# Two transformer layers on one core: the second layer's first attention matrix turned by VectorE and moved by transfers instead of turned by TensorE, with its scores, its bias and an earlier decision moved along

## The chip, the core and the metric

The kernel runs on one core of a Trainium2 chip. The metric is the time of one execution in device microseconds (us). Of the kernel before, three executions gave 462.42, 463.27 and 463.12 us, so the median is 463.12 us. All times of day below ("at 238.47") are microseconds from the start of the profiled execution's span.

## What is computed

Two layers run one after the other on x of 2 sequences x 512 tokens x 512 features. Cut to what matters here:

```python
x = layernorm(x + linear_attention(x))     # 8 heads are read, D = 128
x = layernorm(x + quantised_ffn(x))        # gate, up, down, truncated to int8
# second layer, attention with one head of 128, for each sequence b
qkv  = x @ Wqkv + bqkv ; q, k, v = split(qkv)
attn = softmax((q @ k.T) / sqrt(128))      # 512 x 512 for each sequence
x = layernorm(x + (attn @ v) @ Wo + bo)
x = layernorm(x + swiglu_ffn(x))           # 512 -> 1376 -> 512
```

## The kernel before

**Layout.** A sequence is four tiles of 128 tokens (`xs[b][t]`, 128x512, tokens on partitions). A matmul contracts over partitions, so every time the features or the keys have to stand on partitions a tile is turned. The helper `transposed` (line 118) does that on TensorE: 16 matmuls of 128x128 against the identity into four PSUM tiles (line 128), and four copies to SBUF (line 130), by turns on ScalarE (ACT) and VectorE (DVE). A second way exists in the kernel, `move_squares` (line 286): VectorE first turns every 32x32 square of a tile in place (`nc.vector.transpose`, line 671), and then 16 transfers move the squares to their places, 64 KB each in runs of 128 bytes. Nine of them are issued by SyncE (SP), four by GpSimd (POOL) and three by ScalarE (line 294). The first layer uses it once, for the second sequence's rows (`xt1`).

**PSUM.** There are eight tiles of 128x512 (`psum`). Whoever writes a new one waits for the reader of the one whose place it takes.

**Order.** Instructions of an engine run in order. A scheduler orders all engines but POOL by the program and by what `tc.issue_after` ties; POOL keeps the order of the program. Five places matter here.

1. *Reading the first layer's memory* (lines 548 to 588, and the loop at 674). For each of the 8 token tiles, `read` makes eight matmuls into eight PSUM tiles (`po`, line 557). ACT copies out the denominators (561), VectorE takes their reciprocal (565), ACT scales three of the eight (570) and VectorE adds the other five to x (579). At turns 5 and 6 (counted from 0) TensorE also turns the first sequence's rows (`pt_f`, 275).
2. *The first decision.* Whether the feed-forward weights are ternary is decided by data: `total` sums the counts of misfits at turn 6, and `verdict` (lines 220 to 235) at turn 7 makes a matmul over partitions (`pf_up`, 224) and four small VectorE operations (226, 228, 231, 233). TensorE reads the flag (`branch`, 237), branches (732), and starts the feed-forward matmuls (`pg_f`, 735).
3. *The second attention's projections* (loop at 1012). For sequence 0 and then 1: the rows are turned (`pt_a`, `xt_a`), q and k are projected (`pqk`, 1026) and moved out by ACT (1031), and v is projected (`pv`, 1039) and moved out by VectorE (1043). Behind the turning of sequence 1 stand the splits of the next weights (`split_up`): ACT casts (939, 945) and VectorE differences (953, 954).
4. *Scores and probabilities* (`scores`, `exponentials`). Only after both sequences' projections come the four score matmuls of sequence 0 and the four of sequence 1 (`psc`, 1064), row maxima on VectorE (1070, 1071) and exponentials on ACT (1086).
5. *Turning and using the probabilities.* POOL adds the output bias `bo` to all eight x tiles (1100). TensorE turns sequence 0's probabilities (`pt_p`), `values` (1122) multiplies them by v, then sequence 1's are turned, and `output` (1138), `attended` (1143) and the norms follow.

Between 4 and 5 the kernel before reads:

```python
got, maxima = scores(0)
maxima(range(NT))
got1, maxima = scores(1)
maxima(range(NT - 1))
exponentials(0, got)
for b in range(B):
    for t in range(NT):
        nc.gpsimd.tensor_add(xs[b][t], xs[b][t], bo)
pt0 = transposed(probs[0][0], "p0")
with tc.issue_after(copies[-3].ins):
    scaled_max = maxima([NT - 1])
moved = exponentials(1, got1, {1: copies[-4], 2: copies[-2]})
```

Of the kernel before, what the change touches and what calls it, by code (L numbers as in the profile page):

```python
# [10 lines left out]
F32 = mybir.dt.float32  # L11
# [3 lines left out]
AF = mybir.ActivationFunctionType  # L15
ALU = mybir.AluOpType
# [3 lines left out]
P = 128  # L20
B, S, HID = 2, 512, 512
NT = S // P
NK = HID // P
NH, G, D = 8, 4, 128
# [6 lines left out]
SQ = 32  # L31
# [8 lines left out]
def kernel(  # L40
# [19 lines left out]
    nc = tc.nc  # L60
# [7 lines left out]
    small = ctx.enter_context(tc.tile_pool(name="small", bufs=4))  # L68
# [6 lines left out]
    wqkv = const.tile([P, NK, 3 * D], F32, tag="wqkv", name="wqkv")  # L75
    bv = const.tile([P, D], F32, tag="bv", name="bv")
# [5 lines left out]
    def psum(name):  # L82
        return ps.tile([P, 512], F32, tag="mm", name=name)
# [34 lines left out]
    def transposed(rows, name, in_turn=False):  # L118

        xt = xtp.tile([P, NK, S], F32, tag="xt", name=f"xt_{name}")  # L120
        done = None
        for k in range(NK):
            pt = psum(f"pt_{name}_{k}")
            with ExitStack() as tied:
                if in_turn and k:
                    tied.enter_context(tc.issue_after(done.ins))
                for t in range(NT):
                    done = nc.tensor.transpose(pt[:, ts(t, P)], rows[t][:, ts(k, P)], ident)
            move = nc.vector.tensor_copy if k == 1 or k % 2 > in_turn else nc.scalar.copy
            copies.append(move(xt[:, k, :], pt))  # L130
        return xt
# [209 lines left out]
    def query_tile(name):  # L341
        return wqp.tile([P, 2, HID], F32, tag="wq", name=name)
# [36 lines left out]
    with tc.tile_pool(name="a0w", bufs=1) as a0w, tc.tile_pool(name="a0", bufs=2) as a0:  # L379
# [293 lines left out]
        for i, (b, t) in enumerate(order):  # L673
            steps = read(b, t, lambda steps: norm_a0(i - 1, steps) if i else None)
            for _ in range((1, 1, 1, 1, 1, 1, 0, 0)[i]):
                check_up(*checks.pop(0))
            if i == 6:
                tot_up = total(counts_up[0], "up")
            elif i == 7:
                flag_up, eff_up = verdict(tot_up, sc_up, "up")  # L680
            if i == 5:
                parts, block = split(0)
                x2.append(parts)
                squares = xtp.tile([P, NT, HID], F32, tag="xt", name="squares")
            if i in (5, 6):
                for k in range(2):
                    block(2 * (i - 5) + k)
            if i > NT:
                turn_squares(i - 1)
# [251 lines left out]
    def weight_upper(w, h, name):  # L941

        upper(h, w)
        big = cutp.tile([P, 512], F32, tag="big", name=f"big_{name}")
        nc.scalar.activation(big, w, AF.Copy, scale=BIG)
        return big
# [24 lines left out]
    def take(n):  # L971
        got = free[:n]
        del free[:n]
        return got

    def split_up(j, room, bigs=(None, None)):

        c = turn[j]
        n = CHUNKS[c][1]
        for a in range(2):  # L980
            up_parts[j, a] = room[3 * a : 3 * a + 3]
            if n == P:
                w = gus[c][:, a].rearrange("p k i -> p (k i)")
            else:
                w = gus[c][a]
            if n == P or a == 0:
                done = weight_parts(w, up_parts[j, a], f"gu{j}_{a}", bigs[a])
                continue

            u, w = (v.rearrange("p (k i) -> p k i", k=NK) for v in (up_parts[j, a][0], w))  # L990
            h = u[:, :, : P // 2]
            upper(h, w)
            done = nc.vector.tensor_sub(u[:, :, P // 2 :], w, h.bitcast(F32))
        own = wffn.tile([P, 2 * n // P, 512], F32R, tag=f"gu{c}", name=f"ugu_{c}")
        free.extend(units(own))
        return done
# [8 lines left out]
    def table(func, behind):  # L1005

        with tc.issue_after(behind.ins):
            warm = small.tile([1, 1], F32, tag="warm", name=f"warm_{func.name}", bufs=1)
            nc.scalar.activation(warm, ln_eps[0:1], func)

    qkv = []
    for b in range(B):
        if b:
            xt_a1.append(transposed(xs[b], f"a1{b}"))
            with tc.issue_after(copies[-2].ins), tc.issue_after(copies[-1].ins):
                split_up(0, room0)
                split_up(1, room1[:6])
        xt = xt_a1[b]
        qk = []
        qk2 = query_tile(f"qk_{b}")  # L1020
        if b == 0:
            v2 = query_tile("v")
        for j in range(2):
            p = psum(f"pqk_{b}_{j}")
            for k in range(NK):
                nc.tensor.matmul(  # L1026
                    p, wqkv[:, k, ts(j, D)], xt[:, k, :],
                    start=(k == 0), stop=(k == NK - 1),
                )
            s = qk2[:, j, :]  # L1030
            moved = nc.scalar.activation(s, p, AF.Identity, bias=bqk[:, j : j + 1])
            qk.append(s)
        if b == 0:
            table(AF.Exp, moved)
        v = v2[:, b, :].rearrange("p (t d) -> p t d", t=NT)
        for t in range(NT):
            p = psum(f"pv_{b}_{t}")
            for k in range(NK):
                nc.tensor.matmul(  # L1039
                    p[:, :D], xt[:, k, ts(t, P)], wqkv[:, k, ts(2, D)],  # L1040
                    start=(k == 0), stop=(k == NK - 1),
                )
            nc.vector.tensor_add(v[:, t, :], bv, p[:, :D])
        qkv.append((qk[0], qk[1], v))


    room2 = room1[6:] + take(4)
    with tc.issue_after(moved.ins):
        bigs2 = [
            weight_upper(  # L1050
                gus[turn[2]][:, a].rearrange("p k i -> p (k i)"), room2[3 * a], f"gu2_{a}"
            )
            for a in range(2)
        ]

    probs = []

    def scores(b):

        qt, kt, _ = qkv[b]  # L1060
        got = []
        for t in range(NT):
            p = psum(f"psc_{b}_{t}")
            nc.tensor.matmul(p, qt[:, ts(t, P)], kt, start=True, stop=True)  # L1064
            got.append((p, small.tile([P, 1], F32, tag="mx", name=f"mx_{b}_{t}", bufs=8)))

        def maxima(tiles):
            for t in tiles:
                p, mx = got[t]
                nc.vector.reduce_max(mx, p, AX.X)  # L1070
                done = nc.vector.tensor_scalar_mul(mx, mx, -scale)
            return done

        return got, maxima

    def exponentials(b, got, behind={}):
        sums = small.tile([P, NT], F32, tag="sums", name=f"sums_{b}")
        row = []
        for t, (p, mx) in enumerate(got):
            if t % 2 == 0:  # L1080
                two = pair_tile(f"prob_{b}_{t}")
            e = two[:, t % 2, :]
            with ExitStack() as tied:
                if t in behind:
                    tied.enter_context(tc.issue_after(behind[t].ins))
                moved = nc.scalar.activation(
                    e, p, AF.Exp, bias=mx, scale=scale, accum_out=sums[:, t : t + 1]
                )
            row.append(e)
        probs.append((row, sums))  # L1090
        return moved

    got, maxima = scores(0)
    maxima(range(NT))
    got1, maxima = scores(1)
    maxima(range(NT - 1))
    exponentials(0, got)
    for b in range(B):
        for t in range(NT):
            nc.gpsimd.tensor_add(xs[b][t], xs[b][t], bo)  # L1100
    pt0 = transposed(probs[0][0], "p0")
    with tc.issue_after(copies[-3].ins):
        scaled_max = maxima([NT - 1])
    moved = exponentials(1, got1, {1: copies[-4], 2: copies[-2]})
    table(AF.Silu, moved)
    with tc.issue_after(scaled_max.ins):
        done = split_up(2, room2, bigs2)
    with tc.issue_after(done.ins):
# [6 lines left out]
    def values(b, pt, cuts):  # L1115

        ot = ot2[:, b, :]
        w = S // cuts
        for i in range(cuts):
            po = psum(f"pot_{b}_{i}")  # L1120
            for k in range(NT):
                nc.tensor.matmul(  # L1122
                    po[:, :w], qkv[b][2][:, k, :], pt[:, k, ts(i, w)],
                    start=(k == 0), stop=(k == NT - 1),
                )
            (nc.vector.tensor_copy if b else nc.scalar.copy)(ot[:, ts(i, w)], po[:, :w])
        ots.append(ot)
# [65 lines left out]
        return parts, done  # L1193

    values(0, pt0, 1)
    pt1 = transposed(probs[1][0], "p1")
    for t in range(NT):
        attended(0, t, output(0, t))
        norm_a1(0, t)
# [254 lines left out]
```

## Time and profile before

| what | value |
|---|---|
| median of three executions | 463.12 us |
| the profiled execution's own time | 462.71 us |
| its span, first to last instruction | 460.6 us |
| TensorE matmuls busy | 451.8 us, 98% of the span |
| VectorE busy | 343.1 us, 74% |
| ScalarE busy | 271.4 us, 59% |
| GpSimd busy | 107.1 us, 23% |
| TensorE's part of the chain that ended last | 92% |
| transfers of the core, mean | 76 GB/s |

The profiled execution took 2.1 us more than its span (462.71 less 460.6), and stands 0.4 us below the median. The chain that ended last is followed back from the last instruction; a piece of it is one stretch of time put down to what was then being waited for. In a line of the timeline the first two numbers are the start and the length in us, "x8" is a run of eight instructions merged, and the square brackets give the idle time before it and who ended it.

### The profile page before, as it was taken

How to read it: one execution, taken by the hardware profiler on the slowest of the kernel's cores; microseconds unless marked ns; L12 is line 12 of the kernel's file. 1: busy time of each engine (PE TensorE's matmuls, PEld its weight loads, DVE VectorE, ACT ScalarE, POOL GpSimd, SP SyncE). 2: the span in 40 equal slices, each digit the busy share in tenths (PEclk: the TensorE clock that was granted, in tenths of full speed). 3: DMA queues.
4: the chain of work that ended last, by engine and by line, in shares of the span. 5: the costliest groups of instructions: out<-in, count | busy, mean ns of one | idle time of the engine just before them, and what ended most of it. 6: DMA issues, size and time to landing. Idle time of an engine off the chain costs nothing.

```text
span 460.6 us, 5889 instructions
## 1 busy us (share of the span) xinstructions
PE 451.8 (98%) x1945; PEld 340.4 (74%) x1945; DVE 343.1 (74%) x663; ACT 271.4 (59%) x516; POOL 107.1 (23%) x144
## 2 busy tenths in 40 slices
PE   9999999999899999999999999999999999999994
PEld 8887754344488888888776678888888888888884
DVE  4976857676967878847979899795655878998632
ACT  4778995547467964466755743574755668442101
POOL 0301106566540069101374032000000000020111
PEclk9999999999999999999999999999999999999999
DMA  8999980000038001121580000000000000001101
GB/s 295 395 266 306 183 307 1 0 3 0 2 68 268 5 3 48 47 92 38 196 323 0 2 0 2 0 0 1 0 1 0 1 2 0 1 23 46 38 32 46
DMA packets 21652, 35.03 MB, mean 76 GB/s; under 512 B 9840, under 2 KB 10736, under 8 KB 21616
## 3 DMA queue, kind: packets, MB, share of 16 engines
q1 hardware_dynamic: 18464, 29.54, 18.3%
q0 software_dynamic: 1280, 4.46, 5.0%
q10 hardware_dynamic: 1872, 0.56, 0.5%
q8 instruction: 22, 0.36, 0.3%
q14 instruction: 14, 0.11, 0.1%
HBM read 31.40 MB, written 2.10 MB: 73 GB/s over the span
## 4 chain that ended last, share of the span: by engine, by line
PE 92%; DVE 3%; issue 2%; ACT 1%; POOL 0%; POOLq 0%; DVEq 0%
PE pm L1244 17%; PE po L557 9%; PE pq L502 9%; PE pg_f L735 9%; PE pu_f L735 9%; PE pc L1244 8%; PE pdm L1332 8%; PE pd_f L794 4%; PE pdc L1332 4%; PE pqk L1026 3%; PE pv L1039 2%; PE pot L1122 1%; PE po L1138 1%; PE psc L1064 1%; PE pmw L543 1%
## 5 line engine op out<-in xcount | busy, mean ns | idle before, releaser
L557 PE MATMUL po<-mw,q 128*128 128x512 f32 x128 | 57.0, 598 | 0.6 <-ACT den L561 0.4
L557 PEld LDWEIGHTS po<-mw,q 128*128 128x128 f32 x128 | 22.9, 189 | 33.1 <-issue 18.6
L146 POOL TENSOR_TENSOR rstd_f<-mv_f,ln_eps 128x1 f32<-128x1 f32 x15 | 4.4, 294 | 173.7 <-DVE mv_f L1347 133.2
L1244 PE MATMUL pm<-r,ugu 128*128 128x512 f32 x152 | 37.7, 389 | 0.0
L1244 PE MATMUL pm<-r,it_early 128*128 128x512 f32 x144 | 36.6, 392 | 0.0
L1244 PEld LDWEIGHTS pm<-r,ugu 128*128 128x128 f32 x152 | 28.5, 188 | 5.9
L170 ACT ACTIVATE ta_f<-y_f,below_half 128x512 int8<-128x512 f32 (+1 forms) x22 | 15.9, 721 | 28.5 <-DVE y_f L158 28.2
L1244 PEld LDWEIGHTS pm<-r,it_early 128*128 128x128 f32 x144 | 27.0, 188 | 6.0 <-issue 0.5
L579 DVE SCALAR_TENSOR_TENSOR x<-po,den,x 128x511 f32<-128x511 f32 x40 | 29.8, 745 | 2.0
L1254 DVE SCALAR_TENSOR_TENSOR ev_q<-pm,ev_q 128x512 f32<-128x512 f32 x27 | 18.6, 688 | 14.1 <-PE pm L1244 14.1
L574 POOL TENSOR_TENSOR y<-y,y 128x511 f32<-128x511 f32 x16 | 21.1, 1318 | 26.0 <-PE po L557 21.0
L761 DVE SCALAR_TENSOR_TENSOR it_f<-tb_f,ta_f 128x512 fp32r<-128x512 int16 (+1 forms) x22 | 15.2, 690 | 13.8 <-ACT tb_f L171 13.8
L735 PE MATMUL pg_f<-xh,tu 128*128 128x512 f32 x88 | 24.1, 395 | 1.1 <-ACT den L561 1.1
L1253 ACT ACTIVATE ev_q<-pc 128x512 f32<-128x512 f32 x27 | 16.0, 594 | 14.1 <-PE pc L1244 14.0
L735 PE MATMUL pg_f<-xl,tu 128*128 128x512 f32 x88 | 23.6, 390 | 0.0
L735 PE MATMUL pu_f<-xh,tu 128*128 128x512 f32 x88 | 23.5, 389 | 0.0
L735 PE MATMUL pu_f<-xl,tu 128*128 128x512 f32 x88 | 23.5, 389 | 0.0
L561 ACT ACTIVATE den<-po,den_eps 128x1 f32<-128x1 f32 x64 | 13.9, 278 | 12.5 <-PE po L557 12.4
L349 POOL TENSOR_SCALAR td<-wd,inv_down 128x512 fp32r<-128x512 f32 x11 | 19.8, 1821 | 2.0 <-DVE inv_down L206 2.0
L1134 ACT ACTIVATE x<-x,off_f,rstd_f 128x512 f32<-128x512 f32 x7 | 5.7, 816 | 24.7 <-POOL off_f L1133 24.7
L794 PE MATMUL pd_f<-td,it_f 128*128 128x512 f32 x88 | 20.3, 389 | 0.0
L735 PEld LDWEIGHTS pg_f<-xh,tu 128*128 128x128 f32 x88 | 16.1, 188 | 4.5 <-ACT den L561 1.2
(362 smaller groups left out, 1151.5 us busy)
## 6 DMA issues: line engine op xcount, KB each, us to landing
gu<-in_gu SPq DMA_DIRECT2D x20, 512.0 KB, 6.8
wd<-in_wd SPq DMA_DIRECT2D x20, 256.0 KB, 5.2
wo<-in_wo SPq DMA_DIRECT2D x8, 512.0 KB, 8.3
wo<-in_wo POOLq DMA_DIRECT2D x8, 512.0 KB, 9.9
wq<-in_wq SPq DMA_DIRECT2D x8, 256.0 KB, 4.9
x<-in_x SPq DMA_DIRECT2D x7, 256.0 KB, 4.7
out<-x SPq DMA_DIRECT2D x7, 256.0 KB, 2.0
wqkv<-in_wqkv SPq DMA_DIRECT2D x1, 768.0 KB, 21.6
```

Of the source, the lines that this page charges most:

```text
L170: nc.scalar.activation(a[:n], y, AF.Relu, bias=below_half[:n])
L349: eng.tensor_scalar(out, w, factor, None, ALU.mult)
L502: done = nc.tensor.matmul(p, w, x, start=(start and i == 0), stop=(i == len(todo) - 1), skip_group_check=not start,)
L557: nc.tensor.matmul(po, qs[b][h0 + j][:, ts(t, P)], mw[:, h0 + j, :], start=True, stop=True,)
L574: nc.gpsimd.tensor_add(ys[0][:, :LAST], ys[0][:, :LAST], y[:, :LAST])
L579: steps.append(nc.vector.scalar_tensor_tensor(x[:, :LAST], four[j][:, :LAST], d, x[:, :LAST], ALU.mult, ALU.add))
L735: nc.tensor.matmul(pp[a], t[:, a, i % NK, :], x2[b][i], start=(i == 0), stop=(i == 2 * NK - 1),)
L794: nc.tensor.matmul(pd, inter[b][c][:, ts(t, P)], td[c].bitcast(F32R), start=(c == 0), stop=(c == last),)
L1244: nc.tensor.matmul(p, w, x, start=(left[id(p)] == begun[id(p)]), stop=(left[id(p)] == 1))
L1253: nc.scalar.activation(ev, pc, AF.Copy, scale=CROSS)
L1254: nc.vector.scalar_tensor_tensor(ev, pm, MAIN, ev, ALU.mult, ALU.add)
L1332: nc.tensor.matmul(p[:, :w], got[j // 4][1][kind][:, j % 4], down_parts[j][kind][:, cols], start=(j == 0 and kind == kinds[0]), stop=(j == ...
```

## The change

Sequence 0's scores, maxima and exponentials are made inside the projection loop, straight behind its v. VectorE turns each exponential tile in 32x32 squares, and POOL adds the bias to sequence 0's x tiles there. When the loop comes to sequence 1, `move_squares` is called behind its q and k: 16 transfers write `pt0`. TensorE no longer turns sequence 0's probabilities, so 16 of its transposes and the four copies behind them are gone. Sequence 1's probabilities are still turned by TensorE.

Sequence 1's bias is no longer added by POOL. A POOL copy of one column of `pt0` (`landed`) waits for the move, and behind it POOL issues four transfers that add `bo` from device memory onto the x tiles, 256 KB each.

`values` reads the probabilities with the tokens in four pieces of 128, a row step apart, as `pt0` now has them; `pt1` is given the same form by a view. The ties that interleaved sequence 1's maxima and exponentials with the copies of `pt_p` are gone. And `total` and `verdict` of the first decision come one turn earlier, at turns 5 and 6.

```diff
-            if i == 6:
+            if i == 5:
                 tot_up = total(counts_up[0], "up")
-            elif i == 7:
+            elif i == 6:
                 flag_up, eff_up = verdict(tot_up, sc_up, "up")
...
-        if b == 0:
+        if b:
+            pt0 = fp.tile([P, NT, NK, P], F32, tag="it10", name="pt_p0", bufs=1)
+            move_squares(squares, pt0)
+            pt0 = pt0.rearrange("p t k i -> p k t i")
+        else:
             table(AF.Exp, moved)
...
         qkv.append((qk[0], qk[1], v))
+        if b == 0:
+            got, maxima = scores(0)
+            maxima(range(NT))
+            exponentials(0, got)
+            squares = fp.tile([P, NT, HID], F32, tag="it00", name="squares_p0", bufs=1)
+            for t in range(NT):
+                nc.vector.transpose(squares[:, t, :], probs[0][0][t])
+                nc.gpsimd.tensor_add(xs[0][t], xs[0][t], bo)
...
-    got, maxima = scores(0)
-    maxima(range(NT))
-    got1, maxima = scores(1)
-    maxima(range(NT - 1))
-    exponentials(0, got)
-    for b in range(B):
-        for t in range(NT):
-            nc.gpsimd.tensor_add(xs[b][t], xs[b][t], bo)
-    pt0 = transposed(probs[0][0], "p0")
-    with tc.issue_after(copies[-3].ins):
-        scaled_max = maxima([NT - 1])
-    moved = exponentials(1, got1, {1: copies[-4], 2: copies[-2]})
-    table(AF.Silu, moved)
+    got, maxima = scores(1)
+    scaled_max = maxima(range(NT))
+    table(AF.Silu, exponentials(1, got))
+
+    landed = small.tile([P, 1], F32, tag="landed", name="landed", bufs=1)
+    nc.gpsimd.tensor_copy(landed[2 * SQ : 3 * SQ], pt0[2 * SQ : 3 * SQ, NK - 1, NT - 1, P - 1 :])
+    for t in range(NT):
+        nc.gpsimd.dma_start(xs[1][t], bo_in.to_broadcast([P, HID]), accum_op=ALU.add)
...
                 nc.tensor.matmul(
-                    po[:, :w], qkv[b][2][:, k, :], pt[:, k, ts(i, w)],
+                    po[:, :w].rearrange("p (t i) -> p t i", i=P), qkv[b][2][:, k, :],
+                    pt[:, k, ts(i, NT // cuts)],
                     start=(k == 0), stop=(k == NT - 1),
                 )
...
-    pt1 = transposed(probs[1][0], "p1")
+    pt1 = transposed(probs[1][0], "p1").rearrange("p k (t i) -> p k t i", t=NT)
```

More of the change, by code (lines that the diff above doesn't have):

```diff
@@ L1009, in table @@
             nc.scalar.activation(warm, ln_eps[0:1], func)
-    qkv = []
-    for b in range(B):
[L1013 to L1020, printed above, removed]
-        if b == 0:
[L1022 to L1035, printed above, removed]
-        for t in range(NT):
[L1037 to L1054, printed above, removed]
     probs = []
@@ L1091, in exponentials @@
         return moved
-    got, maxima = scores(0)
-    maxima(range(NT))
-    got1, maxima = scores(1)
-    maxima(range(NT - 1))
-    exponentials(0, got)
-    for b in range(B):
-        for t in range(NT):
-            nc.gpsimd.tensor_add(xs[b][t], xs[b][t], bo)
-    pt0 = transposed(probs[0][0], "p0")
-    with tc.issue_after(copies[-3].ins):
-        scaled_max = maxima([NT - 1])
-    moved = exponentials(1, got1, {1: copies[-4], 2: copies[-2]})
-    table(AF.Silu, moved)
+    qkv = []
+    for b in range(B):
+        if b:
+            xt_a1.append(transposed(xs[b], f"a1{b}"))
+            with tc.issue_after(copies[-2].ins), tc.issue_after(copies[-1].ins):
+                split_up(0, room0)
+                split_up(1, room1[:6])
+        xt = xt_a1[b]
+        qk = []
+        qk2 = query_tile(f"qk_{b}")
+        if b == 0:
+            v2 = query_tile("v")
+        for j in range(2):
+            p = psum(f"pqk_{b}_{j}")
+            for k in range(NK):
+                nc.tensor.matmul(
+                    p, wqkv[:, k, ts(j, D)], xt[:, k, :],
+                    start=(k == 0), stop=(k == NK - 1),
+                )
+            s = qk2[:, j, :]
+            moved = nc.scalar.activation(s, p, AF.Identity, bias=bqk[:, j : j + 1])
+            qk.append(s)
+        if b:
+            pt0 = fp.tile([P, NT, NK, P], F32, tag="it10", name="pt_p0", bufs=1)
+            move_squares(squares, pt0)
+            pt0 = pt0.rearrange("p t k i -> p k t i")
+        else:
+            table(AF.Exp, moved)
+        v = v2[:, b, :].rearrange("p (t d) -> p t d", t=NT)
+        for t in range(NT):
+            p = psum(f"pv_{b}_{t}")
+            for k in range(NK):
+                nc.tensor.matmul(
+                    p[:, :D], xt[:, k, ts(t, P)], wqkv[:, k, ts(2, D)],
+                    start=(k == 0), stop=(k == NK - 1),
+                )
+            nc.vector.tensor_add(v[:, t, :], bv, p[:, :D])
+        qkv.append((qk[0], qk[1], v))
+        if b == 0:
+            got, maxima = scores(0)
[5 more added lines that the diff above has]
+                nc.gpsimd.tensor_add(xs[0][t], xs[0][t], bo)
@@ new lines @@
+    room2 = room1[6:] + take(4)
+    with tc.issue_after(moved.ins):
+        bigs2 = [
+            weight_upper(
+                gus[turn[2]][:, a].rearrange("p k i -> p (k i)"), room2[3 * a], f"gu2_{a}"
+            )
+            for a in range(2)
+        ]
+    got, maxima = scores(1)
[3 more added lines that the diff above has]
+    nc.gpsimd.tensor_copy(landed[2 * SQ : 3 * SQ], pt0[2 * SQ : 3 * SQ, NK - 1, NT - 1, P - 1 :])
```

## The prediction

> **What bounds the kernel now.** Parts 1 and 2 of the page come first.
>
> ```profile
> PE 451.8 (98%) x1945; PEld 340.4 (74%) x1945; DVE 343.1 (74%) x663; ACT 271.4 (59%) x516; POOL 107.1 (23%) x144
> ...
> PEclk9999999999999999999999999999999999999999
> ```
>
> TensorE (PE) is busy throughout at its full clock, so only TensorE's own instructions and its holes set the time. The second view is the chain that ended last (start, length, what), around the two places that the change touches.
>
> ```profile
> 114.72 1.73 PE po L557 x4
> 120.66 1.28 ACT y L570 x3
> 123.14 2.10 PE pg_f L735 x8
> ...
> 236.72 1.75 PE pt_a L128 x16
> 238.47 6.87 PE pqk L1026 x16
> 245.34 3.57 PE pv L1039 x32
> 248.91 6.87 PE psc L1064 x16
> 255.78 1.75 PE pt_p L128 x16
> 257.53 3.44 PE pot L1122 x8
> 260.96 1.75 PE pt_p L128 x16
> ```
>
> From 236.72 to 262.7 each piece begins where the last ended, all of them TensorE's: what is taken from its queue there is gained. At the first place there is a hole before 123.14. The timeline shows it.
>
> ```profile
> 114.93 0.18 DVE L565 RECIPROCAL den<-den 128x4 f32<-128x4 f32 x1 [1.47 <-ACT den L561]
> ...
> 121.72 0.28 PE L224 MATMUL pf_up<-tot_up,ones 128*128 128x1 f32 x2
> 122.31 0.96 DVE L233 TENSOR_SCALAR eff_up<-sc_up,yes_up,no_up 128x2 f32<-128x2 f32 x1
> 123.14 1.18 PE L735 MATMUL pg_f<-xh,tu 128*128 128x512 f32 x4 [1.14 <-ACT den L561]
> ```
>
> The flag's path fills the hole: matmul at 121.72, comparisons on VectorE (DVE), a flag load on TensorE's sequencer at 122.4, a branch, and the next matmul 1.42 after the first. All times below are the old trace's.
>
> **Part 1, the decision a turn earlier: -1.0.** `pf_up` moves in front of the transposes at 113.68 and costs 0.14 of TensorE there. Its five VectorE operations (L226, 228, 231, 233, 717) took 1.34 from 122.04 to the reciprocal at 123.38. They now start about 0.32 behind `pf_up`, at 114.0, and end at 115.34. VectorE idled up to 114.93 anyway (the 1.47 in the first line), so it is only 0.41 late. It has no pause until 121.5, so what is queued behind, the additions of `po` (L579), frees PSUM 0.41 later. The addition that ended at 117.21 now ends at 117.62, and the fourth `po` matmul, which waits for its place, starts at 117.7; five matmuls of 0.86 (two instructions of 0.43) end the turn at 122.0 instead of 121.72. The flag has been ready for 7 us by then. Its load need not wait for the matmuls in front: the third decision's load ran between 197.5 and 197.9 while `pd_f`, the work behind its branch, began at 200.81 without a hole. So `pg_f` starts near 122.1: 1.0 gained. If the load hides only in part, 0.4; with no lateness on VectorE, 1.4.
>
> What follows the earlier start? Sequence 1's feed-forward begins at 145.0 and reads blocks that ACT and VectorE cut from 141.71 to 144.94. A start at 144.0 still finds the upper cuts (done at 143.88), and needs the first lower cut 0.9 later. No new wait; behind it the chain is TensorE's up to 224.
>
> **Part 2, the transposes: -1.75.** One `pt_p` run goes: 16 x 0.109 = 1.75, on the path in full. Its four copies leave ACT and VectorE.
>
> **Part 3, scores in front of sequence 1's rows: +0.5.** Matmuls only change places: `psc` of sequence 0 at 236.72 to 240.16, the rows' transposes to 241.91, then `pqk`. But in the built order ACT does exponentials 0 and 1, copy 0 of the rows, exponentials 2 and 3, copy 2; VectorE squares 0, maxima 2 and 3, squares 1, copy 1, squares 2 and 3, copy 3. `pqk` reads the copies one by one, 0.86 apart. Maximum 0.68 and scaling 0.15 (L1070, L1071), exponential with its sum 0.88 (L1086), one square run 0.71 (L671), copies 0.59 on ACT and 0.69 on VectorE (L130):
>
> - maximum 0 from 237.7, exponential 0 to 239.5, squares 0 to 240.2;
> - maxima 2 and 3 to 241.4, squares 1 to 242.2, copy 1 to 243.0; exponentials 2 and 3 to 243.3, copy 2 to 243.9;
> - squares 2 and 3 to 244.25, copy 3 to 244.9.
>
> `pqk` wants copy 1 at 242.77 and has it at 243.05: 0.3. Copy 3 costs 0.1 to 0.2 more. I take 0.5. Bounds: 0 (if the hand-overs are quicker) and 1.4. The upper one comes from the next lines.
>
> ```profile
> 235.74 11.75 POOL L1100 TENSOR_TENSOR x<-x,bo 128x512 f32<-128x512 f32 x8
> 241.35 1.65 DVE L954 TENSOR_TENSOR it_early<-it_early 128x512 fp32r<-128x512 f32 x1
> 248.56 0.68 DVE L954 TENSOR_TENSOR it_early<-it_early 128x512 fp32r<-128x512 f32 x1
> ```
>
> While GpSimd (POOL) adds the bias, the same VectorE operation takes 1.65 instead of 0.68. Four of the eight adds stay, from 235.74 to about 240.8, beside squares 0: at 1.65 that costs 0.94 more. But the L671 at 112.75 and 120.79 took 0.71 beside POOL adds, and L671 with POOL idle 0.69 to 0.71; so 0.71 it is.
>
> **Part 4, the move of the squares: 0, with 2.2 to spare.** The same move stands in the trace:
>
> ```profile
> L294 SPq DMA_DIRECT2D xt_f<-squares x9: 627/644/1197, 132.2 to 138.8; - x9
> L294 POOL DMA_DIRECT2D xt_f<-squares x4: 666/676/992, 132.7 to 135.0; - x4
> L294 ACTq DMA_DIRECT2D xt_f<-squares x3: 643/654/735, 132.1 to 133.5; - x3
> ...
> DMA to landing us min/median/max: 2.1/3.6/4.9
> ```
>
> Squares done at 132.02 (L671), first reader at 141.71: 9.7 at most, set by SP's nine issues. From 244.25 that is 253.9. The weight loads on the same queues are out of the way: SP's last issue ends at 232.35 and lands some 8.2 later (the median of its six loads there), by 240.6. New is ACT: its three issues stand behind its eight casts and around the two `qk` evictions, the first at about 249.0, the others after 250.0. SP's ninth waits, in the built program, for ACT's first to land: 251.2, so it issues by 251.9 and lands by 254.1. `pot` starts when `psc` of sequence 1 ends, 240.16 + 1.75 + 6.87 + 0.5 + 3.57 + 3.44 = 256.3. Without that cover each us late costs one. ACT's issues (3 x 0.65) and POOL's (4 x 0.68) lie beside TensorE's work.
>
> The Trainium skill ("VectorE: DVE Perf Modes", "The three transpose paths" and "Rules for kernel authors") says that VectorE turns only 32x32 blocks and advises TensorE for a 128x128 transpose where PSUM will do; taken as a rule for this case the sum would be no gain, not -1.75, but it weighs the operation alone, not which engine bounds. The skill ("DMA: Bandwidth & Descriptors", "Specifications") asks for 512 bytes or more for full transfer rate and the runs here have 128, while its section "Why small descriptors are slow (HBM only)" exempts moves within SBUF; by either, the 9.7 above already holds the price, so the sum stays.
>
> **Part 5, the strided `values`: 0.** No row has 512 columns in four pieces. Nearest: `pv`, 128 columns an instruction, 0.112 each (3.57 / 32), 0.446 for 512 against 0.430 (3.44 / 8). So 0 to +0.13; contiguous runs of 512 bytes are nearer to 0.
>
> **Part 6, sequence 1's bias: 0.** `landed` holds POOL until 254.1; its next work is the norm at 265.97 (L146). Four issues of 0.86, 1.27 apart as in the L606 run at 44.12, end by 259. The POOL loads of part 6 landed in 9.9 at twice the size: x tiles complete from 264.3 to 268.1. `attended` reads them (L1143) at 270.56, 271.42, 272.28 and 275.21, now about 1.2 earlier in this stage's terms. Nothing waits; a shortfall would cost its own length.
>
> Behind `pot` VectorE and ACT have less than before (copies gone, maxima done), and the holes between 274 and 298, VectorE's row splits, stay.
>
> **Sum.** -1.0 - 1.75 + 0.5 = -2.25. The span goes from 460.6 to 458.35, the profiled execution from 462.71 to 460.46. That execution was 0.4 below the median, so I forecast 463.12 - 2.25 = **460.9**; its own range is 460.0 to 461.7 (parts 1 to 3 at their nearer ends).
>
> **Rivals.**
> 1. *The decision gains nothing.* The part of the change that doesn't do what it says: VectorE's lateness reaches the last `po` and the load stays exposed. For it: L233 took 0.96 beside a POOL add and a POOL add runs at 113.94 too. Against it: the third decision. -1.25: 461.9.
> 2. *The row copies are late.* Squares 0 at 1.65 gives +1.4 in part 3, and the decision only 0.4: -0.4 - 1.75 + 1.4 = -0.75: 462.4, within what can't be told from none.
> 3. *The move lands late: slower.* Place: the first `pot` matmul, waiting for SP's ninth transfer, which waits for ACT's first. If the eight splits run at 1.65, as five did in this trace, ACT's casts, which wait for them, let the first ACT issue out at about 254.4 (+5), SP's ninth lands near 259.5 and `pot` waits 3.2; `qk` of sequence 1 is late for `psc` by some 2 of these. With the rest of the sum: -2.25 + 3.3 = +1.05, 464.2. It decides from 5.4 us of lateness on (2.2 to spare, 2.25 gained, 0.93 to count as slower); below 4.45 the change still gains. For it: a queue of waits that the earlier move, issued by idle engines, never had. Against: POOL has stopped adding by 241, and rows without POOL show 0.68.
>
> **Chances.** Forecast 0.56, rival 1 0.14, rival 2 0.14, rival 3 0.16. A difference under 0.2% (0.93 us) can't be told from none here. So faster (below 462.2) 0.70, same 0.14, slower 0.16. The range reaches from the forecast with all of part 1 and no stall (-3.2: 459.9, and 459.8 with the spread of the runs) past rival 2 to the middle between it and rival 3: 463.0.
>
> **What would show it.** Right: one `pt_p` run fewer, no piece but TensorE's between `psc` and `pot`, `pg_f` directly behind the last `po`, and holes of some 0.3 in the second `pqk`. Wrong: `pot` waiting for a transfer, `psc` for ACT's `qk`, L671 over 1 us, or L1143 waiting for POOL's queue.

## The result and the profile after

The changed kernel takes **465.59 us** (median of six executions, 465.43 to 466.13), the kernel before beside it 463.19 (six, 462.42 to 464.31). The ratio is 1.0051, 95% interval 1.0038 to 1.0065: slower by 2.4 us where a gain of 2.25 was forecast. The profiled execution took 466.13, with a span of 464.4, where that of before had 460.6.

The two rows of the page that were shown of before, now of the kernel after:

```profile
PE 456.6 (98%) x1929; PEld 338.2 (73%) x1929; DVE 340.1 (73%) x665; ACT 270.6 (58%) x514; POOL 107.2 (23%) x149
...
PEclk9999999999999999999999999999999999999999
```

TensorE has 16 instructions fewer, as meant, at the same clock. Yet it is busy 4.8 us longer (456.6 for 451.8). That one row holds the case: the time was not lost in a wait.

The chain of the kernel after at the first place (start, length, what):

```profile
115.00 0.13 PE pf_up L224 x2
...
115.49 0.92 DVE eff_up L233
...
116.58 0.10 DVE den L565
...
118.85 4.53 PE po L557 x10
123.38 1.84 PE pg_f L735 x8
```

The hole is gone: the decision is made on VectorE by 116.58, seven us ahead, and `pg_f` follows the last `po` at once. From the chain's first `po` (64.08, in before 62.91) to its first `pg_f` it took 59.30 instead of 60.23.

The same chain around the second attention:

```profile
226.62 1.75 PE pt_a L128 x16
...
238.80 3.44 PE psc L1019 x8
242.24 1.75 PE pt_a L128 x16
243.98 7.03 PE pqk L1063 x16
...
254.59 3.44 PE psc L1019 x8
258.02 3.43 PE pot L1129 x8
261.45 1.75 PE pt_p L128 x16
```

One `pt_p` run is gone, `pot` follows `psc` without a wait, and the second `pqk` takes 7.03 instead of 6.87. From the first `pt_a` to the end of the first `pot` it is 34.83 us (226.62 to 261.45), in before 36.58 (224.38 to 260.96); 0.15 of these 1.75 are the first `pt_a` (1.75 for 1.90), so the change itself gained 1.6: 1.75 less the 0.16.

So both places gained, 0.93 and 1.6, and yet the span grew by 3.8. The loss is in pieces that nobody touched. One piece of the chain in the kernel before:

```profile
200.81 4.99 PE pd_f L794 x22
```

and the same 22 matmuls in the kernel after:

```profile
202.37 5.13 PE pd_f L794 x22
```

A run of 22 fp32r matmuls of 128x512 takes 5.13 instead of 4.99: 5.13 / 22 = 233 ns from start to start instead of 227. This holds nearly everywhere, also in the feed-forward of the first layer (an L735 run of eight: 1.85 or 1.86, in before 1.81), far ahead of the attention that was changed, and behind it (`pdm` x22: 5.11, in before 4.99). Matmuls of full fp32 kept their time (`psc`, eight in 3.44). From the first `pg_f` to the second layer's `pt_a` the kernel after needs 103.24 us instead of 101.24, and from the attention's last `po` (end at 275.27, in before 274.78) to the end of the last matmul 183.47 instead of 179.94: 5.5 us lost, more than was gained.

### The profile page after: what moved, and what is told of

The parts are those of the page before. It is cut to its first block, busy times and chain, and to the rows that moved or that the text cites. A ratio compares the mean times of both kernels' runs of the same rounds, so it can differ in the third digit from the quotient of the medians.

```text
span 464.4 us, 5879 instructions
## 1 busy us (share of the span) xinstructions
PE 456.6 (98%) x1929; PEld 338.2 (73%) x1929; DVE 340.1 (73%) x665; ACT 270.6 (58%) x514; POOL 107.2 (23%) x149
## 4 chain that ended last, share of the span: by engine, by line
PE 92%; DVE 3%; issue 2%; DMA 1%; ACT 1%; SPq 0%; POOL 0%; POOLq 0%; DVEq 0%
PE pm L1252 18%; PE po L557 10%; PE pq L502 9%; PE pg_f L735 9%; PE pu_f L735 9%; PE pc L1252 8%; PE pdm L1340 8%; PE pd_f L794 4%; PE pdc L1340 4%; PE pqk L1063 3%; PE pv L1080 2%; PE pot L1129 1%; PE po L1146 1%; PE psc L1019 1%; PE pmw L543 1%
## 5 line engine op out<-in xcount | busy, mean ns | idle before, releaser
L735 PE MATMUL pg_f<-xh,tu 128*128 128x512 f32 x88 | 24.8, 404 | 0.0
L735 PE MATMUL pu_f<-xh,tu 128*128 128x512 f32 x88 | 24.1, 396 | 0.0
L735 PE MATMUL pu_f<-xl,tu 128*128 128x512 f32 x88 | 23.9, 393 | 0.0
L735 PE MATMUL pg_f<-xl,tu 128*128 128x512 f32 x88 | 23.8, 392 | 0.0
L1252 PE MATMUL pc<-r,ugu 128*128 128x512 f32 x72 | 19.7, 395 | 0.0
```

Of the source, the lines that this page charges most:

```text
L735: nc.tensor.matmul(pp[a], t[:, a, i % NK, :], x2[b][i], start=(i == 0), stop=(i == 2 * NK - 1),)
L1252: nc.tensor.matmul(p, w, x, start=(left[id(p)] == begun[id(p)]), stop=(left[id(p)] == 1))
```

## The experiments

**Theory A** after this comparison: the new tile `landed` is the cause, by its place in memory. In the built program it takes 32 bytes of each partition, and 361 tiles allocated behind it, weights and activations of the fp32r matmuls among them, lie 32 bytes higher than in the kernel before. **Theory B**: the new order, the transfers or POOL's work slow the matmuls. **Theory C**: it was the chip or the execution. Ratios below are to the kernel before on the same chip, whose median was 463.2 to 463.6.

### same

The kernel before once more.

> The kernel before, unchanged. Theory A (addresses): untouched fp32r matmuls of 512 columns start 227 ns apart as in the first profile of it (pd_f x22 in 4.99 us), about 463.2 us. Theory C (the chip or the execution gave the slow pace): about 232 ns apart here too, and then every kernel of this call shows it.

Measured: 464.19 us, span 462.1. `pd_f` x22 took 4.99 again, so C falls. The span is 1.5 longer than in the first profile; 1.05 of it lies between the first `po` and the first `pg_f`, where one `po` waited 0.5 for ACT's `y` (L570). One profile alone thus tells stages of the first layer to no better than about 1 us.

### aligned

```diff
-    landed = small.tile([P, 1], F32, tag="landed", name="landed", bufs=1)
+    landed = small.tile([P, 16], F32, tag="landed", name="landed", bufs=1)
...
```

POOL's copy in the next line now names the tile's first column.

> The changed kernel with the tile landed 64 bytes a partition instead of 4. In the built programs every engine has the same instructions in the same order; only the 361 tiles that are allocated behind landed lie 64 bytes higher than in the kernel before, where the change put them 32 bytes higher. Theory A (the 32 bytes slow the matmuls): the pace returns to 227 ns (pd_f x22 in 4.99 us instead of 5.13), and what is left is the saving of the decision (0.93) and of the transposes (1.75): 463.2 - 2.7 = 460.5 us. Theory B (the new order, its transfers or POOL's work slow the matmuls): no change, 465.6 us.

Measured: 465.74 us, ratio 1.0042 (1.0028 to 1.0056); `pd_f` x22 5.13. My size for theory A was wrong: 64 bytes are no better than 32. By itself this run favours B.

### shift

```diff
+    landed = small.tile([P, 1], F32, tag="landed", name="landed", bufs=1)
+    nc.gpsimd.memset(landed, 0.0)
     pt0 = transposed(probs[0][0], "p0")
```

> The kernel before, with one 4-byte tile added (landed, cleared once by POOL behind its bias adds); nothing else. The same 361 tiles lie 32 bytes higher. Theory A: the pace goes to 231 to 235 ns from the first quarter of the kernel on, some +5 to +6 us: 468 to 469 us. Theory B: 463.2 us, no difference.

Measured: 469.77 us, ratio 1.0130 (1.0113 to 1.0147): +6.2 us. The same piece of the chain in this kernel:

```profile
203.66 5.13 PE pd_f L794 x22
```

To a hundredth the piece of the kernel after (and `pdm` x22 has 5.11 here too), in a program that is the kernel before plus four bytes a partition. So the slow pace does not need B, and A stands, but not with a boundary of 64 bytes.

Setting the addresses of the operands in the built program beside the pace gave **theory D**. In the kernel before, the two operands of 1,264 of the 1,371 fp32r matmuls of 512 columns start a multiple of 512 bytes apart, those of the other 107 an odd multiple of 256 (the expectation of reuse below says 512 of all). In the kernel after, 811 of them stand 32 bytes off this. A long stretch where both operands had moved by 32 ran at 227 ns (1.81 / 8, from 310.19 to 315.6 on the chain), and those where only one had moved at 231 to 235.

```profile
310.19 0.91 PE pc L1252 x4
311.10 1.81 PE pm L1252 x8
```

So what counts is where the moving operand and the stationary operand lie *to each other*.

### reuse

```diff
-    landed = small.tile([P, 1], F32, tag="landed", name="landed", bufs=1)
+    landed = small.tile([P, 1], F32, tag="off", name="landed")
```

> The changed kernel with landed put into a place that the kernel already has (the small tile off of the norms), so that no tile of an fp32r matmul lies elsewhere than in the kernel before; the same instructions in the same order as the changed kernel. Theory D (the pace depends on where the moving operand and the stationary operand lie to each other: 227 ns where their addresses differ by a multiple of some power of two above 64 bytes, as all do in the kernel before by multiples of 512, and some 232 ns otherwise): pace 227, time 463.3 - 0.9 - 1.75 = 460.6 us or a little below. Theory B (the change's own order or transfers slow the matmuls as well): between 462 and 465.6.

Measured: **460.54 us**, ratio 0.9927 (0.9905 to 0.9948). The piece of its chain:

```profile
200.61 4.99 PE pd_f L794 x22
```

The same instructions in the same order as in the kernel after, 5 us faster by the place of one small tile. With this B is out.

### pad128 and pad512

```diff
-    landed = small.tile([P, 1], F32, tag="landed", name="landed", bufs=1)
+    landed = small.tile([P, 32], F32, tag="landed", name="landed", bufs=1)    # pad512: [P, 128]
...
```

> The changed kernel with landed of 128 bytes a partition; 361 tiles lie 128 bytes higher than in the kernel before, instructions and order as in the changed kernel. Theory D with a period of 128 bytes: pace 227, 460.6 us. With a period of 256 or more: 231 to 234 ns, about 465.6.

> As before with 512 bytes a partition. Theory D: 227 ns and 460.6 us, since every difference of addresses is again a multiple of 512. If any added memory costs, whatever its size: about 465.6.

Measured: pad128 465.40, ratio 1.0040 (1.0025 to 1.0055), `pd_f` x22 5.11; pad512 **459.91**, ratio 0.9922 (0.9895 to 0.9949), `pd_f` x22 4.99. It is not added memory that costs, but an addition that is no multiple of the period, and the period is above 128.

### micro

> Leaves the whole computation out: 13 stretches of 48 fp32r matmuls of 128x512, four stationary blocks in turn, nothing beside them; the output is one moved-out result for each tile, not the layers'. The stationary operand lies 0, 4, 16, 32, 64, 128, 256, 512, 96 bytes off the moving operand's place modulo 512; then both 32 off, the moving alone 32 off, the moving by turns 0 and 32 off; then 0 again. Theory D: 227 ns from start to start at 0, 512, 0 again and both 32 off (10.9 us a stretch of 48), 230 to 235 ns (11.1 to 11.2 us) at 32, 64, 96, moving alone and by turns; 4 and 16 as 32, 128 and 256 tell the period. If other engines' accesses are needed for the slow pace: 227 ns in all of them.

The timeline of TensorE in this kernel (start, length, and the tile named after the offset; in the `b_` stretch both operands are 32 bytes off, in `m_thirtytwo` the moving one alone, in `m_turns` every second moving one):

```profile
19.06 11.32 PE L83 MATMUL s_four<-mov,sta 128*128 128x512 f32 x48
30.21 11.36 PE L83 MATMUL s_sixteen<-mov,sta 128*128 128x512 f32 x48
41.41 11.35 PE L83 MATMUL s_thirtytwo<-mov,sta 128*128 128x512 f32 x48
52.60 11.36 PE L83 MATMUL s_sixtyfour<-mov,sta 128*128 128x512 f32 x48
63.80 11.32 PE L83 MATMUL s_onetwoeight<-mov,sta 128*128 128x512 f32 x48
74.96 11.05 PE L83 MATMUL s_twofivesix<-mov,sta 128*128 128x512 f32 x48
85.84 11.05 PE L83 MATMUL s_fivetwelve<-mov,sta 128*128 128x512 f32 x48
96.73 11.07 PE L83 MATMUL b_thirtytwo<-mov,sta 128*128 128x512 f32 x48
107.64 11.36 PE L83 MATMUL m_thirtytwo<-mov,sta 128*128 128x512 f32 x48
118.84 11.20 PE L83 MATMUL m_turns<-mov,sta 128*128 128x512 f32 x48
129.88 11.40 PE L83 MATMUL s_ninetysix<-mov,sta 128*128 128x512 f32 x48
141.12 11.05 PE L83 MATMUL s_again<-mov,sta 128*128 128x512 f32 x48
```

Read the starts, since the ends overlap: a stretch's start to the next one's, over 48. At 256 bytes (85.84 - 74.96) / 48 = 227 ns, at 512 and with both operands moved 227 also; at 32 bytes (52.60 - 41.41) / 48 = 233, at 64 also 233, at 128 232.5; the offsets of 4, 16 and 96, by the same reckoning, 232, 233 and 234. By turns it is 230, between the two. No other engine takes part but for one copy a stretch, so it is TensorE's own two operands. (The very first stretch, at offset 0, began with matmuls 427 ns apart and is left out; the last one, `s_again`, repeats it and takes 11.05, as at 256 and 512.)

This settles the cause. A period of 256 bytes fits every offset that was tried, and theory D's price fits: in the kernel after some 1,330 consecutive pairs of such matmuls were 3 to 6 ns above 227 on average by their class of offset, 6.5 us in all, and shift measured 6.2.

Not all of this falls on operands that lie apart. In 530 of these pairs the moving operand lies 0 or 256 from its own weights and from the next ones, as in the kernel before, and yet they start 230 ns apart on average: 1.6 of the 6.5 us. Most of them stand in short runs between the others. Micro shows that the pace can take some matmuls to settle after a change of place: the first starts of `b_thirtytwo` are 230, 224, 231, 236, 228, 233, 231 and 226 ns apart, and from there on nearly all 227 or 226 (in `s_again` only the first, 231, stands out). The same series is in the kernel after: of the `pc` and `pm` from 297.02 on whose two operands both stand 32 off, the starts are 230, 236, 228, 233, 231, 226, 227 and 227 apart. That the 1.6 us are this settling is likely, not shown.

### decision, squares, poolbias

These three size the parts of the change with the addresses of the kernel before. decision is the kernel before with the decision alone a turn earlier:

```diff
-            if i == 6:
+            if i == 5:
                 tot_up = total(counts_up[0], "up")
-            elif i == 7:
+            elif i == 6:
```

> The kernel before, with the first decision alone one turn earlier; all addresses as before. From the trace of the changed kernel: the time from the first po to the first pg_f falls from 60.23 to 59.30 us, so 463.2 - 0.9 = 462.3 us. If the gain is given back behind it: 463.2.

Measured: 462.35 us, ratio 0.9976 (0.9965 to 0.9986): -1.1 us. squares is the kernel reuse with these two lines turned back.

> The kernel reuse (addresses as in the kernel before) with the first decision back at turns 6 and 7: parts 2 to 6 of the change alone. If these parts bring what they are forecast, less the stall that was 0.16 in the trace of the changed kernel: 463.5 - 1.75 + 0.15 = 461.9 us, and the difference to reuse is the decision, 0.9 to 1.2. If the two parts are not additive (a hole that only appears without the other): outside 461.5 to 462.3.

Measured: 461.08 us, ratio 0.9952 (0.9938 to 0.9966): -2.2 us, with 1.6 to 2.9 in the interval. The parts add up: 0.9976 x 0.9952 = 0.9928, and reuse has 0.9927.

```diff
-    landed = small.tile([P, 1], F32, tag="off", name="landed")
-    nc.gpsimd.tensor_copy(landed[2 * SQ : 3 * SQ], pt0[2 * SQ : 3 * SQ, NK - 1, NT - 1, P - 1 :])
     for t in range(NT):
-        nc.gpsimd.dma_start(xs[1][t], bo_in.to_broadcast([P, HID]), accum_op=ALU.add)
+        nc.gpsimd.tensor_add(xs[1][t], xs[1][t], bo)
```

> The kernel reuse with sequence 1's bias added by POOL (four adds behind its four issues of the move) instead of by transfers; landed is gone. If VectorE's splits beside POOL's adds have room: 460.5, no difference to reuse. If they cost as in rival 3 of the prediction: the adds run from about 246.5 to 252.4, four or five of VectorE's splits (L953, L954) beside them take 1.65 instead of 0.69, VectorE ends 3.9 to 4.8 later, of which it has some 2.6 free before sequence 1's first maximum; the rest, 1.3 to 2.2, delays the exponentials and with them pt_p: 461.8 to 462.7.

Measured: 460.97 us, ratio 0.9948 (0.9934 to 0.9961); its interval overlaps that of reuse, so the times do not tell the two apart. The profiles do. VectorE's timeline in poolbias:

```profile
244.19 0.69 DVE L954 TENSOR_TENSOR it_early<-it_early 128x512 fp32r<-128x512 f32 x1
244.79 3.44 DVE L953 SCALAR_TENSOR_TENSOR it_early<-it_early,big_gu 128x512 fp32r<-128x512 f32 x2
```

POOL's four adds run from 245.87 to 252.72, and the five splits beside them, of which the second line has the first two, take 1.72 to 1.75 instead of 0.69. The chain runs through them into the exponentials and from the last of these, over ACT's function load (L1009, 1.28) and its copy of `ot`, to the `po` of the attention, which waits 0.34 for it. From the first `pt_a` of the second layer to its first `pm` it is 49.60 us, in reuse 48.81: the transfers save 0.8 of the attention's time, where I had expected 1.3 to 2.2.

## Why the prediction was wrong

**The step that failed is part 6**, "Sequence 1's bias: 0", and behind it the first part's "only TensorE's own instructions and its holes set the time". I priced `landed` as time on POOL ("holds POOL until 254.1") and in POOL's time it was right: the four issues ran from 256.42 to 260.05, and the first reader, at 270.99, did not wait for them. I did not ask where its four bytes lie. They moved one operand of 811 of the 1,371 fp32r matmuls of 512 columns by 32 bytes against the other. The sum had taken it for granted that matmuls which the change does not touch keep their 227 ns; by their class of offset they took 3 to 6 ns more on average, in all +6.2 us (shift). None of the rivals held that; the one that ended slower put the loss into a late transfer. With it the account closes: 0.9927 (reuse) x 1.0130 (shift) = 1.0056, against 1.0051 measured.

The other steps, in their order:

- **Part 1** (-1.0): right. -1.1 by decision (-0.6 to -1.6); the -0.93 between two traces alone would not carry it, since one profile tells this stage to no better than 1 us (same). The way was also as described: five VectorE operations end at 116.58, 1.58 behind the start of `pf_up`; the `po` run behind them starts at 118.85 after a wait of 0.15 for VectorE; and the flag's load shows nowhere. Rival 1 is out.
- **Part 2** (-1.75): right, the run of 16 is gone.
- **Part 3** (+0.5): 0.16, nearer to its lower end. The chain above has 7.03 for 6.87. VectorE's squares took 0.71 and less, as chosen, not 1.65. Rival 2 is out.
- **Part 4** (0, with 2.2 to spare): right. The transfers into `pt0` in the kernel after:

```profile
L294 SPq DMA_DIRECT2D pt_p<-squares_p x9: 606/642/1768, 245.9 to 253.4; - x9
...
L1110 POOL COPY landed<-pt_p x1: 180/180/180, 255.9 to 255.9; 32x1 f32<-32x1 f32 x1
```

  The squares were done at 245.83 (the last two, 244.54 and 1.29 long); POOL's copy of the landed column started 10.0 later, at 255.85 (forecast 9.85, 244.25 to 254.1), and `pot` wanted it at 258.02: 2.2 to spare. Rival 3 did not come, since VectorE's splits took 0.69 once POOL had stopped adding. What it said of those splits is true where POOL does add: poolbias.
- **Part 5** (0): right, `pot` x8 in 3.43, in before 3.44.
- **The sum** (-2.25) for these parts: reuse has -3.4 (-2.4 to -4.4), pad512 -3.6 (-2.4 to -4.9). The forecast of 460.9 would have been near for either (460.54 and 459.91), a little too high; but it starts from 463.12, and beside these two the kernel before took 463.55, so part of that nearness is luck. Of what is missing the profiles show 0.34 in part 3 and some 0.3 behind the last matmul (span's end less the last matmul's: 5.61 in reuse, 5.91 in before; also 5.62 in squares, but 5.95 in decision and 6.06 in poolbias); the rest, some 0.5, is within the interval. Why the end is shorter in the kernels with the bias's transfers no run shows. The prediction's top bound is also misworked: the middle between rivals 2 and 3 (462.4 and 464.2) is 463.3, not 463.0.

The Trainium skill ("VectorE: DVE Perf Modes", "Rules for kernel authors"), which the prediction set against this change since it advises TensorE for a 128x128 transpose, is answered by squares: -2.2 us here for parts 2 to 6 together, because TensorE's queue bounds the kernel and VectorE's and the queues' time was free.

## What to carry to other kernels

Look at the busy time of an engine whose work did not change: if it grew without a wait, compare the start-to-start time of untouched instructions before looking at the edit. Where TensorE bounds, as here, a new tile need not be free however small, for it can move all tiles allocated behind it (361 here); put it into a place that exists, or round it to 512 bytes as pad512 did. And price an edit by what it does to memory too, not only by engines, queues and waits.

## What the runs showed of the hardware that was not expected

Back-to-back fp32r matmuls of 128x512, each with new weights, start 227 ns apart when the moving and the stationary operands lie 0, 256 or 512 bytes from each other in the partition (modulo 512), and 232 to 234 ns apart (2 to 3% slower) at offsets of 4, 16, 32, 64, 96 and 128 bytes. The common place does not matter (both 32 off: 227), with every second moving operand off it is 230, and after a change of place up to eight starts came 224 to 236 apart before the pace settled (`b_thirtytwo`). Whether a matmul is held up by its own weights or by the loading of the next ones, these runs do not tell.

Two kinds did not lose. Eight matmuls of full fp32 (`po` of the second attention, its two operands 32 bytes off in the kernel after) take 3.44 us in the kernels after and reuse alike. And the fp32r matmuls of 256 columns start 118 ns apart at the median in the kernel after (117 where their operands lie 32 apart), 120 in the kernel before: a little faster.

The Trainium skill ("SBUF — State Buffer", "Operand start alignment") lets an fp32 operand start at any multiple of 4 bytes and says that this is about legality and that nothing was timed. The runs here are such a timing for TensorE's two operands: not all of those starts are equally fast.
